# Graph attention, then neighbour quantiles, on one core: the order of scatters, of front pieces and of the first indices is changed

## The chip, the cores and the metric

The kernel runs on one core of a Trainium2 chip. That core has five engines, each with an instruction queue of its own that is worked off in order: TensorE (PE in the profile, its weight loads PEld), VectorE (DVE), ScalarE (ACT), GpSimd (POOL) and SyncE (SP). Transfers between HBM and the on-chip memories are issued from a queue of SP, ACT or POOL. The metric is the device time of one execution in microseconds (us). Semaphores order the engines; a framework places them from the tiles that instructions read and write, and also chooses, at compile time, the order of instructions in each queue.

## The reference, cut to what matters

Two layers follow each other. The first is dense graph attention with 8 heads on 4096 nodes of 128 values, masked by an adjacency matrix of about 1.6% ones, then an output projection and a layer norm:

```python
Wh = jnp.einsum('nd,hde->hne', nodes, W)
e = leaky_relu(f1[:, :, None] + f2[:, None, :])        # f1, f2: Wh times a1, a2
att = softmax(where(adj > 0, e, -9e15))
h = elu(einsum('hnm,hmd->hnd', att, Wh))
x = layernorm(nodes + elu(cat(h) @ W1 + b1))           # (4096, 128)
```

The second layer takes, for each node and each of the 128 features, the three quartiles over the values of the node's neighbours (of which a few, by rank, are left out), averages them, mixes them half and half with the node's own value, and applies one linear layer with a residual:

```python
svals = jnp.sort(where(keep[:, :, None], x[None], big), axis=1)
agg = sum(take(svals, ceil(q * n_keep) - 1) for q in (0.25, 0.5, 0.75)) / 3
out = (0.5 * agg + 0.5 * x) @ W.T + b + x
```

## The kernel before

The kernel makes use of the sparse graph: a node has some 50 to 100 neighbours. Nodes are handled 128 at a time (32 tiles), one per partition. There are three kinds of work.

**The front** (`Front`, from L318) turns the adjacency matrix into lists. `scan` loads quarter rows (`a_i`, 512 KB, SP's queue, L378), ScalarE makes signs of them, TensorE packs 16 columns into a word. `first` and `second` (DVE: rounds of eight maxima and their replacement, L188 and L190) draw the neighbours' numbers out of the words. Tiles come in six blocks of 4, 4, 6, 6, 6 and 6 (`BLOCKS`). `place` sorts the nodes of a block by their degree: it computes a place for each node (`pos_i`, L518), and POOL scatters the lists to those places in HBM (`rows_d`, L541). `keep` writes a row `meta_d` of indices for the second layer. At the end, `order` computes the places over all 4096 nodes, and `late`, 32 scatters from POOL of 512 bytes each, writes `order_d` (L680). The front is cut into 88 pieces in a list `todo`; `advance(n)` takes the next n, and `through(b)` all up to the `place` of block b.

**Attention** (`gat`, from L797) goes in 64 halves of 64 nodes. A node has 8 partitions, so a half is 4 groups of 16 nodes. For each group, gathers from POOL (`nb`, L971) of 128 rows of 136 values each, 28 to 44 gathers for a half and 2190 in all, bring the neighbours' rows from `xf_d`; their indices come from `rows_d` through `ids`, `others` and `info` on SP. Gathers are issued three halves ahead, into six buffers of 18 rows. DVE and ACT make logits and probabilities (L1054 to L1088), DVE spreads them (L1103), TensorE sums the rows (`ps_z`, L1111), and every four halves `combine` computes projection, `elu` and layer norm, one stage of it in each of the halves that follow. It ends in two scatters of the result into `x1_d` (L1197), which the profile calls `x_d`. Each half of the loop ends with `advance(2)`. The loop takes `late` in behind the last gather of the program's text, but a scatter of `late` depends on the front alone, so the framework may place it earlier.

**Quantiles** (`sparse`, from L1675) go by tiles of 128 nodes, sorted by degree. POOL fetches the tile's `info` row, the nodes' own values `xs`, and 50 to 100 neighbour rows (`rows`, L1713; three tiles of buffers). DVE sorts the rows with a network of compares (`compare`, L1738). A compare of k pairs is one ACT copy of the lower rows to PSUM (tile `low`, two of them[...]; up to 4 pairs to `low_s` in SBUF) at L1751, then a minimum and a maximum on DVE (L1756, L1757). `interleave` orders the steps of the end of tile t-1 and the beginning of tile t. `plan` makes the steps, of at most 16 pairs, 8 in the first part of tile 0. When a tile is sorted, `pick` lets ACT scale 2 to 14 candidate rows (`picked`, L1810), lets TensorE sum them into the last quarter of a `low` tile that a compare of at most 12 pairs is using (`sums`, L1815 and L1818), and ACT copies the sum out. Every fourth tile, `finish` does the linear layer likewise (`layer`, L1837) and scatters the output. These small jobs stand in the list `waiting`; each compare takes one.

Between the two layers, a flag is read and a branch taken: a graph that doesn't fit the bounds takes a dense path. Nothing after the branch is placed ahead of it.

Of the kernel before, what the change touches and what calls it, by code (L numbers as in the profile page):

```python
# [38 lines left out]
F32 = mybir.dt.float32  # L39
F16 = mybir.dt.float16  # L40
BF = mybir.dt.bfloat16
I32 = mybir.dt.int32
# [3 lines left out]
ALU = mybir.AluOpType  # L46
# [4 lines left out]
P = 128  # L51
N = 4096
D = 128
# [36 lines left out]
SMALL = 4  # L90
FOUR = 4
CUT = 32
MOST = 16

ENDS = [(t - t % FOUR, FOUR) for t in range(NT - FOUR)]
ENDS += [(NT - FOUR, FOUR - 1)] * (FOUR - 1) + [(NT - 1, 1)]
# [697 lines left out]
    return out  # L794


def gat(tc, nc, c, x, adj, xf_d, meta_d, order_d, flag_d, w, a1, a2, w1, b1, gamma, beta, x1_d):  # L797

# [22 lines left out]
    with ExitStack() as ctx:  # L823
# [3 lines left out]
        def advance(count):  # L827
            while todo and count > 0:
                name, piece = todo.pop(0)
                piece()  # L830
                count -= name != "open"
# [299 lines left out]
        def combine(t, zT):  # L1131
# [62 lines left out]
            nc.vector.tensor_add(s, s, bc["beta"].unsqueeze(1).to_broadcast(shape))  # L1194
            yield
            for j in range(TWO):
                nc.gpsimd.indirect_dma_start(  # L1197
                    out=x1_d,
                    out_offset=bass.IndirectOffsetOnAxis(ap=index[t + j][3][:, 0:1], axis=0),
                    in_=s[:, j, :],  # L1200
                    in_offset=None,
                )

        held = {u: load(u) for u in range(3)}
        advance(EARLY)
        f1s = {0: spread_f1(0)}
# [3 lines left out]
        for u in range(2 * NT):  # L1210
            t, half = divmod(u, 2)
            if u + 3 < 2 * NT:
                held[u + 3] = load(u + 3)
            elif late:

                advance(len(todo))
                for piece in late:
                    piece()
                late = []
            if not half and t + 1 < NT:  # L1220
                f1s[t + 1] = spread_f1(t + 1)
            ps_z, behind = rows_sum(u, held.pop(u), e)
            if u + 1 < 2 * NT:
                with ExitStack() as order:
                    for ins in behind:
                        order.enter_context(tc.issue_after(ins))
                    e, behind = probabilities(u + 1, held[u + 1], f1s[(u + 1) // 2])
            with ExitStack() as order:
                for ins in behind:
                    order.enter_context(tc.issue_after(ins))  # L1230
                if u % (2 * TWO) == 0:
                    zT = tp.tile([P, H, TWO * P], F32, name="zT")
                collect(u, ps_z, zT)
                for stages in going:
                    next(stages, None)
            if u % (2 * TWO) == 2 * TWO - 1:
                going = going[-1:] + [combine(t - 1, zT)]
            advance(2)
        for stages in going:
            for _ in stages:  # L1240
                pass
        advance(len(todo))


def statistics(tc, nc, c, f_sb, f2m, rows_d):
# [412 lines left out]
def plan(t):  # L1658

    wide = HIGH[t]  # L1660
    extra = wide - MAIN if MAIN < wide <= 80 else 0
    w = wide - extra
    needed = {i - 1 for lo, hi in places(t) for i in range(lo - extra, hi + 1)}
    layers = needed_swaps(swap_layers(w), needed)
    merge = (w - 1).bit_length()

    first = steps(layers[:-merge], lambda i: i, PAIRS if t else PAIRS // 2)
    second = steps(layers[-merge:], lambda i: i)
    if extra:
        apart = needed_swaps(swap_layers(extra), range(extra))  # L1670
        first += steps(apart, lambda i: MAIN + extra - 1 - i)
    return first, second, extra


def sparse(tc, nc, c, x1_d, meta_d, order_d, w, b, out):  # L1675


    with tc.tile_pool(name="sp1", bufs=1) as one, tc.tile_pool(
# [12 lines left out]
        sixth = one.tile([P, P], F32, name="sixth_i")  # L1691
        nc.scalar.mul(sixth, c["idf"], 0.5 * float(np.float32(1.0 / NQ)))
        wT = one.tile([P, D], F32, name="lwT")
        it = one.tile([P, 2 * MIDDLE], I32, name="it_p")
        nc.gpsimd.iota(it, pattern=[[1, 2 * MIDDLE]], base=0, channel_multiplier=0)
        iota_p = one.tile([P, 2 * MIDDLE], F32, name="iota_p")
        nc.vector.tensor_copy(iota_p, it)
        order = one.tile([P, NT], I32, name="order")
        for i in range(4):
            nc.sync.dma_start(  # L1700
                out=order[:, ts(i, NT // 4)],
                in_=order_d[ts(i, N // 4), :].rearrange("(t p) c -> p (t c)", p=P),
            )

        def bank():
            return psum.tile([P, PAIRS * D], F32, name="low")

# [2 lines left out]
        nc.scalar.copy(wT, ps[:, :D])  # L1710

        def gather(row, info, col):
            nc.gpsimd.indirect_dma_start(  # L1713
                out=row,
                out_offset=None,
                in_=x1_d,
                in_offset=bass.IndirectOffsetOnAxis(ap=info[:, col : col + 1], axis=0),
            )
# [19 lines left out]
        def compare(rows, step):  # L1738


            shape, d, low, high, _ = step
            lows, highs = block(rows, shape), block(rows, shape, d)
            if low and high:
                _, n2, _, n, _, run = shape
                k = n2 * n * run
                if k > SMALL:
                    t = bank()
                else:
                    t = tp.tile([P, SMALL * D], F32, name="low_s", bufs=4)
                packed = block(t, (0, n2, n * run, n, run, run))  # L1750
                nc.scalar.copy(packed, lows)  # L1751
                if waiting and waiting[0][0] == "copy":
                    waiting.pop(0)[1]()
                elif waiting and SMALL < k <= PAIRS - FOUR:
                    waiting.pop(0)[1](t[:, (PAIRS - FOUR) * D :])
                nc.vector.tensor_tensor(lows, packed, highs, op=ALU.min)  # L1756
                nc.vector.tensor_tensor(highs, packed, highs, op=ALU.max)  # L1757
            elif low:
                nc.vector.tensor_tensor(lows, lows, highs, op=ALU.min)  # L1759
            else:  # L1760
                nc.vector.tensor_tensor(highs, lows, highs, op=ALU.max)
# [41 lines left out]
        def pick(found, x1, comT):  # L1803

            made = {}

            def scale():
                made["v"] = tp.tile([P, MOST, D], F32, name="picked", bufs=1)
                for i, (v, weight) in enumerate(found):
                    nc.scalar.mul(made["v"][:, i, :], v, weight)  # L1810

            def sums(ps):
                made["ps"] = ps[:, :P]
                for i in range(len(found)):
                    nc.tensor.matmul(  # L1815
                        made["ps"], made["v"][:, i, :], sixth, start=i == 0, stop=False
                    )
                nc.tensor.matmul(made["ps"], x1, half, start=False, stop=True)  # L1818

            return [  # L1820
                ("copy", scale),
                ("bank", sums),
                ("copy", lambda: nc.scalar.copy(comT, made["ps"])),
            ]

        def finish(xs, comT, infos):
# [3 lines left out]

            def layer(ps):
                made["ps"] = ps
                for j in range(m):
                    to = ps[:, ts(j, D)]
                    nc.tensor.matmul(to, c["idf"], xs[:, j, :], start=True, stop=False)
                    nc.tensor.matmul(to, c["ones"][0:1, :], b_row[:, j, :], start=False, stop=False)
                    nc.tensor.matmul(to, comT[:, j, :], wT, start=False, stop=True)  # L1837

            def layer_copy():
                o = tp.tile([P, FOUR, D], F32, name="o")  # L1840
# [15 lines left out]
        def load(t):  # L1856
            rows = three.tile([P, max(HIGH), D], F32, name="rows")
            first, _ = ENDS[t]
            if t == first:
                group[first] = (  # L1860
                    tp.tile([P, FOUR, D], F32, name="xs"),
                    tp.tile([P, FOUR, P], F32, name="comT"),
                    [],
                )
            info = three.tile([P, MW], I32, name="info", bufs=3 * FOUR)
            group[first][2].append(info)
            nc.gpsimd.indirect_dma_start(
                out=info,
                out_offset=None,
                in_=meta_d,  # L1870
                in_offset=bass.IndirectOffsetOnAxis(ap=order[:, t : t + 1], axis=0),
            )
            gather(group[first][0][:, t - first, :], info, NODE)
            for s in range(HIGH[t]):
                gather(rows[:, s, :], info, s)
            return rows, info

        plans = [plan(t) for t in range(NT)]
        held = {0: load(0), 1: load(1)}
        for t in range(NT + 1):  # L1880
# [372 lines left out]
def gnn(tc, x, adj, w, a1, a2, w1, b1, gamma, beta, lw, lb, out):  # L2253
    nc = tc.nc
    with ExitStack() as ctx:
# [6 lines left out]

        keep = ctx.enter_context(tc.tile_pool(name="keep", bufs=1))
        c = constants(nc, keep)
        gat(tc, nc, c, x, adj, xf_d, meta_d, order_d, flag_d, w, a1, a2, w1, b1, gamma, beta, x1_d)
        other = nc.values_load(flag_d[0:1, 0:1], min_val=0, max_val=1)
        with tc.If(other > 0) as cmp:
            general(tc, nc, c, x, adj, w, a1, a2, w1, b1, gamma, beta, lw, lb, x1_d, out)
        with cmp.Else():
            sparse(tc, nc, c, x1_d, meta_d, order_d, lw, lb, out)  # L2270


_INS = [
# [33 lines left out]
```

## Time and profile before

| | us |
|---|---|
| timed runs, median of 3 | 8430.65 (8417.16 to 8433.3) |
| profiled execution | 7646.96 |
| its span, from the first to the last instruction | 7645.2 |
| places of the first block ready, first gathers | 133 |
| end of the last gather of attention | 3106.6 |
| last scatter of `x1_d` issued | 3158.4 |
| first row gather of quantiles | 3170.6 |
| first compare | 3187.1 |
| last scatter of the output | 7641 |

The profiled execution is 784 us shorter than the median of the timed runs. All durations that follow are those of the profiled execution. A line of a group of instructions gives the line in the kernel, the engine, the operation and the tiles it writes and reads; a waiting row gives what waited for what, us in total, times, and the longest. The releaser of a wait is inferred. Idle time counts only on the engine that bounds a stage.

### The profile page before, as it was taken

Reading aid. Unit: us, or ns where it says so; the run is one execution under the profiler, and the core shown is the slowest. Engines: PE = TensorE matmul, PEld = TensorE weight load, DVE = VectorE, ACT = ScalarE, POOL = GpSimd, SP = SyncE. Lnnn points to the kernel's source line nnn. Section 1 sums busy time; section 2 is a strip of 40 time slices with the busy share of each in tenths; the row PEclk is TensorE's granted clock in tenths of the full one; section 3 lists DMA queues with packets and bytes.
Section 4 is the critical chain, followed back from the end, with each engine's and each line's share of the span. In section 5 each row is a group of like instructions: output and inputs, shape, how many; then the busy total and the mean of one; then the engine's idle time right before and its main releaser. Section 6 shows DMA issues by size and latency. Waiting matters only on the chain. (4 is left out here: it accounts for less than half of the span.)

```text
span 7645.2 us, 31290 instructions
## 1 busy us (share of the span) xinstructions
PE 1122.8 (15%) x6047; PEld 946.8 (12%) x6047; DVE 5831.7 (76%) x9380; ACT 2214.1 (29%) x2301; POOL 4343.5 (57%) x4524
## 2 busy tenths in 40 slices
PE   3243333322222322100000000000000000000001
PEld 1232222222222222100000000000000000000000
DVE  8465555565223222399999999999999999999999
ACT  6020212100000000144344343434334433443433
POOL 2777677777777777565554645455536434554500
PEclk5566666666566666655555555555555555555555
DMA  6242324222222222111111111111101101111100
GB/s 205 57 121 56 107 62 121 60 55 56 47 56 56 56 56 56 40 44 34 40 35 30 41 31 37 30 36 34 38 23 41 34 24 33 36 35 29 33 1 1
DMA packets 219057, 380.95 MB, mean 50 GB/s; under 512 B 129283, under 2 KB 129412, under 8 KB 218852
## 3 DMA queue, kind: packets, MB, share of 16 engines
q0 software_dynamic: 145808, 308.58, 15.3%
q1 hardware_dynamic: 72898, 70.23, 3.1%
q14 instruction: 156, 1.28, 0.1%
q8 instruction: 49, 0.80, 0.0%
q10 hardware_dynamic: 146, 0.07, 0.0%
HBM read 368.26 MB, written 10.31 MB: 50 GB/s over the span
## 5 line engine op out<-in xcount | busy, mean ns | idle before, releaser
L1713 POOL DMA_INDIRECT rows<-x_d,info x2078 | 2018.2, 971 | 1949.5 <-ACT picked L1810 1270.8
L971 POOL DMA_INDIRECT nb<-xf_d,ids x2190 | 2086.0, 953 | 707.0 <-issue 632.2
L1751 ACT COPY low<-rows 128x2048 f32<-128x2048 f32 (+8 forms) x1022 | 1561.5, 1533 | 2429.9 <-DVE rows L1757 1780.7
L1756 DVE TENSOR_TENSOR rows<-low,rows 128x2048 f32<-128x2048 f32 (+9 forms) x1022 | 1884.7, 1862 | 138.9 <-ACT low L1751 50.0
L1757 DVE TENSOR_TENSOR rows<-low,rows 128x2048 f32<-128x2048 f32 (+9 forms) x1022 | 1882.4, 1861 | 5.8
L1054 DVE TENSOR_TENSOR e<-nb,ps_small 128x64 f32<-128x64 f32 (+9 forms) x200 | 47.7, 240 | 1252.6 <-DMA nb<-xf_d,ids 1206.7
L1111 PE MATMUL ps_z<-spread,nb 128*128 128x128 f32 x4500 | 615.7, 305 | 797.9 <-DVE spread L1103 775.6
L1111 PEld LDWEIGHTS ps_z<-spread,nb 128*128 128x128 f32 x4500 | 604.5, 220 | 829.9 <-DVE spread L1103 420.7
L1815 PE MATMUL low<-sixth_i,picked 128*128 128x128 f32 x300 | 79.8, 442 | 4224.7 <-ACT low L1751 3736.4
L1815 PEld LDWEIGHTS low<-sixth_i,picked 128*128 128x128 f32 x300 | 66.8, 324 | 4237.7 <-ACT low L1751 3744.8
L1073 ACT ACTIVATE ps_e<-e 128x256 f32<-128x256 f32 (+4 forms) x64 | 26.1, 408 | 1936.2 <-DVE e L1054 972.6
L1103 DVE TENSOR_TENSOR spread<-e,ps_small 128x1152 f32<-128x1152 f32 (+4 forms) x312 | 342.7, 1107 | 129.2 <-PE ps_z L1111 79.4
L1845 POOL DMA_INDIRECT out<-o,info x32 | 34.4, 1076 | 392.9 <-ACT o L1841 369.2
L380 ACT ACTIVATE nz<-a_i 128x1024 bf16<-128x1024 int32 x128 | 134.3, 1051 | 292.5 <-DMA a_i<-in_adj 254.3
L1751 ACT COPY low_s<-rows 128x512 f32<-128x512 f32 (+3 forms) x325 | 139.8, 471 | 130.5 <-DVE rows L1756 48.0
L389 PE MATMUL ps_words<-nz,pows 128*128 128x512 bf16 (+1 forms) x272 | 113.7, 577 | 364.4 <-ACT nz L387 258.0
L188 DVE MAX8 k<-key 128x8 f32<-128x256 f32 x416 | 164.6, 412 | 0.7
L1756 DVE TENSOR_TENSOR rows<-low_s,rows 128x512 f32<-128x512 f32 (+3 forms) x325 | 158.3, 500 | 3.0 <-ACT low_s L1751 2.1
L1757 DVE TENSOR_TENSOR rows<-low_s,rows 128x512 f32<-128x512 f32 (+3 forms) x325 | 158.7, 500 | 0.3
L190 DVE MATCH_REPLACE8 key<-k,key 128x256 f32<-128x256 f32 x384 | 155.5, 407 | 0.0
L1142 PE MATMUL ps_h<-zT,w_ga 128*128 128x256 f32 x256 | 116.3, 619 | 198.4 <-DVE s L1414 106.6
L1759 DVE TENSOR_TENSOR rows<-rows 128x256 f32<-128x256 f32 (+8 forms) x245 | 141.6, 580 | 0.2
(246 smaller groups left out, 2528.0 us busy)
## 6 DMA issues: line engine op xcount, KB each, us to landing
a_i<-in_adj SPq DMA_DIRECT2D x128, 512.0 KB
nb<-xf_d,ids POOLq DMA_INDIRECT x2190, 2.5
rows<-x_d,info POOLq DMA_INDIRECT x2078, 2.5
xf_d<-xf POOLq DMA_DIRECT2D x4, 576.0 KB, 7.4
xf<-in_x POOLq DMA_DIRECT2D x4, 512.0 KB
meta_d<-rowdata_k SPq DMA_DIRECT2D x4, 324.0 KB
abc_ta<-in_L_gnn_a POOLq DMA_DIRECT2D x2, 512.0 KB, 7.7
w_ga<-in_L_gnn_W POOLq DMA_DIRECT2D x2, 512.0 KB
```

Source lines behind the costliest of these rows:

```text
L188: nc.vector.max(out=top, in_=work)
L190: nc.vector.match_replace(out=work, in_to_replace=top, in_values=work, imm_value=gone)
L380: nc.scalar.activation(nz[:, j, :], a_i, AF.Relu, scale=-1.0, accum_out=self.negative[:, k : k + 1],)
L971: gather = nc.gpsimd.indirect_dma_start(out=rows[:, used + i, :], out_offset=None, in_=xf_d, in_offset=bass.IndirectOffsetOnAxis(ap=ids[:, ...
L1103: last = nc.vector.tensor_tensor(spread[:, :m], e[:, at : at + m, :].unsqueeze(2).to_broadcast(shape), own.unsqueeze(1).unsqueeze(3).to_br ...
L1111: product = nc.tensor.matmul(ps_z[:, g, :], rows[:, k, :D], spread[:, i].rearrange("p j h -> p (j h)"), start=i0 + i == 0, stop=i0 + i == ...
L1713: nc.gpsimd.indirect_dma_start(out=row, out_offset=None, in_=x1_d, in_offset=bass.IndirectOffsetOnAxis(ap=info[:, col : col + 1], axis=0),)
L1751: nc.scalar.copy(packed, lows)
L1756: nc.vector.tensor_tensor(lows, packed, highs, op=ALU.min)
L1757: nc.vector.tensor_tensor(highs, packed, highs, op=ALU.max)
L1759: nc.vector.tensor_tensor(lows, lows, highs, op=ALU.min)
L1815: nc.tensor.matmul(made["ps"], made["v"][:, i, :], sixth, start=i == 0, stop=False)
```

## The change

- The 32 scatters of `late` are put behind the last gather of attention on POOL.
- The scatters into `x1_d` no longer wait for one another; each node has a row of its own.
- `advance` takes three pieces at the end of each of the first 16 halves, two thereafter.
- `order` and the first two `info` rows are loaded inside `gat`, between the last but one and the last `combine`, into tiles that outlive it; so is the constant `iota_p`. `sparse` no longer makes them.
- In the first part of tile 0, steps have at most 4 pairs instead of 8.
- A compare no longer depends on the matmuls of `sums` or `layer` that use other columns of its PSUM tile.
- `scale` is one piece for each row instead of one for all.
- In `load` of quantiles, everything stands behind the row gathers of the tile before, `xs` behind the rows; `info` has 10 buffers instead of 12, and `picked` 14 rows instead of 16.

```diff
@@ gat
             for j in range(TWO):
-                nc.gpsimd.indirect_dma_start(
+                done = nc.gpsimd.indirect_dma_start(
                     out=x1_d,
...
                 )
-
+                for other in stored:
+                    tc.declare_no_dep(done.ins, other, reason="each node has a row of its own")
+                stored.append(done.ins)
...
                 advance(len(todo))
-                for piece in late:
-                    piece()
+                with tc.issue_after(gathers[2 * NT - 1][HALF - 1, 0]):
+                    for piece in late:
+                        piece()
                 late = []
...
-            advance(2)
-        for stages in going:
+            advance(3 if u < 2 * START[2] else 2)
+        for stages in going[:-1]:
             for _ in stages:
                 pass
-        advance(len(todo))
+
+        for i in range(4):
+            nc.sync.dma_start(
+                out=order[:, ts(i, NT // 4)],
+                in_=order_d[ts(i, N // 4), :].rearrange("(t p) c -> p (t c)", p=P),
+            )
+        for t, info in enumerate(infos):
+            nc.gpsimd.indirect_dma_start(
+                out=info,
+                out_offset=None,
+                in_=meta_d,
+                in_offset=bass.IndirectOffsetOnAxis(ap=order[:, t : t + 1], axis=0),
+            )
+        for stages in going[-1:]:
+            for _ in stages:
+                pass
@@ plan
-    first = steps(layers[:-merge], lambda i: i, PAIRS if t else PAIRS // 2)
+    first = steps(layers[:-merge], lambda i: i, PAIRS if t else PAIRS // 4)
@@ sparse, compare
+                aside = []
                 if waiting and waiting[0][0] == "copy":
                     waiting.pop(0)[1]()
                 elif waiting and SMALL < k <= PAIRS - FOUR:
-                    waiting.pop(0)[1](t[:, (PAIRS - FOUR) * D :])
-                nc.vector.tensor_tensor(lows, packed, highs, op=ALU.min)
-                nc.vector.tensor_tensor(highs, packed, highs, op=ALU.max)
+                    aside = waiting.pop(0)[1](t[:, (PAIRS - FOUR) * D :])
+                for to, op in ((lows, ALU.min), (highs, ALU.max)):
+                    done = nc.vector.tensor_tensor(to, packed, highs, op=op)
+                    for product in aside:
+                        tc.declare_no_dep(done.ins, product, reason="other columns of the bank")
@@ sparse, load
-            info = three.tile([P, MW], I32, name="info", bufs=3 * FOUR)
-            group[first][2].append(info)
-            nc.gpsimd.indirect_dma_start(
...
-            gather(group[first][0][:, t - first, :], info, NODE)
-            for s in range(HIGH[t]):
-                gather(rows[:, s, :], info, s)
+            with ExitStack() as after:
+                if gathered:
+                    after.enter_context(tc.issue_after(gathered[-1]))
+                if t < len(infos):
+                    info = infos[t]
+                else:
+                    info = three.tile([P, MW], I32, name="info", bufs=2 * FOUR + 2)
+                    nc.gpsimd.indirect_dma_start(
...
+                for s in range(HIGH[t]):
+                    done = gather(rows[:, s, :], info, s)
+                gather(group[first][0][:, t - first, :], info, NODE)
+                gathered.append(done.ins)
```

`tc.issue_after(ins)` puts the instructions of its block behind `ins` in the same engine's queue; `tc.declare_no_dep(a, b)` takes away the dependence of `a` on `b`.

## The prediction

> **What bounds the kernel now.** I read the page first, then the stage table, then the waits of the bounding engine in each stage, then the timeline of the crossing between them.
>
> The page's slices show two regimes: VectorE partly idle in the first 17, full in the rest.
>
> ```profile
> PE 1122.8 (15%) x6047; PEld 946.8 (12%) x6047; DVE 5831.7 (76%) x9380; ACT 2214.1 (29%) x2301; POOL 4343.5 (57%) x4524
> ...
> DVE  8465555565223222399999999999999999999999
> ...
> POOL 2777677777777777565554645455536434554500
> ```
>
> In the stage table (stretch, length, then busy time and count for PE, PEld, DVE, ACT, POOL):
>
> ```profile
> 1911.00:3049.00 1138.00, 313.16 (x1989) 290.53 (x1987) 313.30 (x802) 67.41 (x127) 860.05 (x910) 0.62 0.23 55
> 3310.00:7500.00 4190.00, 136.54 (x488) 110.90 (x488) 4098.18 (x3180) 1673.71 (x1437) 2000.71 (x2055) 0.50 0.12 32
> ```
>
> Attention late on: 910 POOL instructions in 1138 us, 1.25 us each. The timeline has each gather busy 0.94 and idle 0.30 "issue", so POOL is full at 76% busy: attention ends when the gathers have been issued, plus the stalls of POOL. Quantiles: DVE is 97.8% busy. Time comes out of this kernel by taking an instruction or a stall from POOL before the last gather, by shortening the crossing, or by closing DVE's last gaps.
>
> POOL's stalls in attention (waited for: total us, times, longest):
>
> ```profile
> POOL nb L971 <- PE ps_z L1111: 36.9, 8, 21.6
> ...
> POOL me L947 <- DMA info<-rows_d: 12.3, 3, 4.2
> ...
> POOL x_d L1197 <- DMA x_d<-s,info: 10.6, 6, 3.2
> ```
>
> The first is a gather waiting for a buffer because VectorE is late. Why it is late shows in SyncE's timeline and in DVE's waits at the same place:
>
> ```profile
> 778.87 4.17 SPq L903 DMA_DIRECT2D ids<-rows_d  x6
> 783.08 5.75 SPq L919 DMA_DIRECT2D others<-rows_d  x11
> 788.94 19.71 SPq L378 DMA_DIRECT2D a_i<-in_adj  x8
> ```
> ```profile
> DVE ps_e L1074 <- ACT ps_e L1073: 39.4, 1, 39.4
> ```
>
> SP stood at `ids` until POOL's scatters of block 2 (770 to 778), though their places were ready at 711; the adjacency pieces queued behind came at 789; ScalarE, in order, held a scan ahead of the logits; DVE lost 39 us, then POOL 8.5 and 21.6 us.
>
> The crossing:
>
> ```profile
> 3105.62 0.94 POOL L971 DMA_INDIRECT nb<-xf_d,ids  x1 [0.30 <-issue]
> ...
> 3146.65 0.98 POOL L1197 DMA_INDIRECT x_d<-s,info  x1 [40.09 <-DVE s L1194]
> ...
> 3158.36 0.96 POOL L1197 DMA_INDIRECT x_d<-s,info  x1 [2.55 <-DMA x_d<-s,info]
> ...
> 3162.97 0.99 POOL L1867 DMA_INDIRECT info<-meta_d,order  x1 [0.72 <-issue]
> ...
> 3170.57 0.94 POOL L1713 DMA_INDIRECT rows<-x_d,info  x1 [0.30 <-issue]
> ...
> 3187.05 0.96 DVE L1756 TENSOR_TENSOR rows<-low,rows 128x768 f32<-128x768 f32 x1 [20.10 <-DMA rows<-x_d,info]
> ```
>
> From the last gather's end (3106.6) to the first row gather of quantiles: 64.0 us, in which POOL sits idle for 40.
>
> DVE's gaps after 3310:
>
> ```profile
> DVE rows L1756 <- ACT low L1751: 44.9, 45, 1.9
> DVE rows L1756 <- PE low L1837: 20.3, 8, 3.3
> DVE rows L1756 <- PE low L1818: 12.3, 10, 2.2
> ```
>
> [...] the matmuls of `sums` and `layer` write its last quarter and the compare beside them uses 12 rows, the first three. So the 18 waits above (32.6 us) order things that needn't be, and I count them as gone. [...] the forecast for attention goes by where instructions stand in each queue.
>
> **The change part by part**, against the profiled execution (7646.96 us, span 7645.2). The median of the timed runs is 8430.65, 784 us more; nothing in this trace says where that lies.
>
> (1) Late scatters. In the order before, all 32 of `order_d` stand between gathers 1297 and 1347 of 2190; in the changed order, behind the 2190th. They cost POOL 32 x 1.256 = 40.2 us ahead of the last gather; there they now stand in the 40.1 us hole. Gain 40.
>
> (2) Free scatters of `x_d`. The second of each pair waited 1.53 us, where 0.30 is normal: eight such in attention, with one of 3.2, make some 10 us.
>
> (3) Three pieces per half in the first 16 halves. No work is added; DVE's front work moves earlier, and the POOL order with it. I gave each DVE instruction of the changed order the mean by which its kind advances DVE in this trace, and counted POOL's at 1.249 us from the first scatter at 133:
> - block 1: DVE needs 122 us, POOL arrives after 207;
> - block 2: DVE 196 more, POOL 229 later (scatter behind gather 333, at 569);
> - block 3: DVE 200 more, POOL 237 later (behind gather 507, at 807);
> - blocks 4 and 5: DVE 207 and 233, POOL 295 and 336.
>
> So DVE keeps up, at 86% where it is tightest (62% before). Its in-order waits matter too: the places of block 2 come 57 us of DVE work behind the logits of half 7, whose gathers end at about 497: 558, against 569. Those of block 3 come 55 us behind half 13 (gathers end 750): 806, against 807. I allow 3 us there. Behind a waiting scatter stand all later gathers, and on SP `ids` and the adjacency pieces, so this is the place to watch. In return the scatters come when their places are ready, rather than 59 us later (block 2), and SP lets the scan through: pieces issued behind block 2's scatter are needed by half 10, whose gathers end only at 617. Of the 36.9 us of buffer stalls I keep 6: gain 31. The waits of 4.1 us for `info` follow a pair of stores on which SP waits to refill that buffer; two of three stay: gain 4.
> Sum for attention: 40 + 10 + 31 + 4 - 3 = 82 us. From both sides: 40 (each stall comes back as another) to 100; and below nothing, see the rivals.
>
> (4) Indices ahead. The 32 scatters end 40 us after the last gather, land 3.6 later (median of that DMA), the loads of `order` take SP 2.4 and then some 2.4 to land (taken from `info`, the nearest row), the two `info` gathers 2.5, and four stores, whose last values are ready at 48, 5: 54 to 56 instead of 52.8. Then the branch (2.7) and rows at once; five `info`, one `xs` and the iota (8 us) are gone: 58 instead of 64. Gain 6. If that cover were gone (stores ready sooner), the chain through `order` would be late next.
>
> (5) First tile in steps of 3 or 4 pairs: the first compare needs 6 rows, not 12: 7.5 us sooner. But its last row lands 62 us after its first in either kernel, and tile 1's rows, which DVE met 2 us after they landed, become the next limit. Gain 5, between 0 and 8; the steps add some 4 us of DVE work inside waits.
>
> (6) The 18 waits for PE: gain 30 of 32.6. Between 0 and 33: ACT's copy out of the bank could take the wait over, but DVE is two compares, over 4 us, away from that bank.
>
> (7) Scaling piece by piece, `xs` and `info` behind the rows, buffers 12 to 10, MOST 14: nothing. ACT's order of scales and copies is almost the same in both, so row buffers come free at the same points; POOL has a mean 45 us of idle (1270.8 / 28) ahead of each tile's gathers, and rows land 17 us or more before first use in all but tiles 1 and 31. If the releases did come one compare (4.4 us) later, tile 31 would feel it alone.
>
> Sum: 82 + 6 + 5 + 30 = 123: 7524 in a profile. If the 784 us of the timed runs stretch all stages alike (1.10), it is 135. I take 130: 8300.
>
> **Rivals.**
> (A) Attention wins only the scatters and half the stores' waits (45): a buffer stall or a wait at `rows_d` of 30 to 40 us replaces the old ones. For it: margins of 1 and 11 us at two scatters. Against: DVE has 155 us unused before block 3's. Gain 86: 8345. Chance 0.22.
> (B) Attention as forecast, the PE waits return as waits for ACT: gain 93: 8338. For it: the ACT row is already the largest. Chance 0.12.
> (C) Slower: DVE's idle share doesn't shrink. From 133 to 711 it was busy 347.5 of 578 us. If it idles 40% on, its 518 us of work take 863, block 3's places come at 996 instead of 806, POOL stalls 190 us at that scatter, and the time is 8430.65 + 190 - 123, about 8500. It decides once the two stalls at blocks 2 and 3 pass 123 us together. Against: part of that idling was the blocked scan, which goes, and the rest was VectorE waiting for gathers with no front piece placed ahead. Chance 0.09, of which 0.04 stalls that just eat the gain.
> (D) The timed runs lose more than the profile where POOL bounds, and gains there grow: 8250. Chance 0.10.
> (E) The change does not do what it says, the scatters still ahead of the gathers or on the way out: the order of instructions excludes the first; the second costs at most the 40, gain 83, 8348. Chance 0.05.
> The forecast, 8275 to 8325, has 0.42.
>
> **Numbers.** Time 8300; range 8245 to 8375, which leaves out the tail of D and C. A measurement of this kernel can tell about 0.2% (17 us). Faster 0.91, same 0.04, slower 0.05.
>
> **What would show it.** Last gather near 3025 (3107 before); no `order_d` scatter among gathers; no wait of `x_d` for `x_d`; POOL's wait at `rows_d` under 15 us for blocks 2 and 3 (more says A or C); rows of tile 0 begin 58 us after the last gather; the two rows "<- PE low" gone from DVE's waits and the ACT row no larger than 50 (else B). The forecast is wrong if DVE's front work meets POOL at the scatters, or if the unseen 784 us depend on the order of transfers.

## The result and the profile after

The changed kernel is slower: 8545.69 us (median of 4 runs, 8537.73 to 8555.35) against 8431.97 for the kernel before on the same chip, ratio 1.0138 (95% interval 1.0120 to 1.0156), 114 us. The forecast was 8300.

One thing has to be said for the numbers to be understood: the kernel before takes 7643 to 7655 us in some sessions on a chip and 8377 to 8440 in others (one chip showed both), all kernels of a session move together, the profile that the forecast was made from is of the first kind and the timed runs given with it of the second. I call them the 7647 setting and the 8430 setting, and compare only with the kernel before in the same session.

The profile after is of the 8430 setting (span 8535.9 us). The page, busy time first, then the slices:

```profile
PE 1224.0 (14%) x6047; PEld 1018.7 (12%) x6047; DVE 5890.0 (69%) x9454; ACT 2221.7 (26%) x2338; POOL 4346.9 (51%) x4524
...
DVE  6454564553222222225898979899899998999999
...
POOL 3545546566666666656254534536454435444410
```

Busy times are those of the kernel before within some 100 us; the span is not. VectorE is no longer at 9 in every slice of the quantiles, and POOL no longer at 7 in attention. The stage table, with the same two stretches as in the prediction:

```profile
1911.00:3049.00 1138.00, 344.37 (x1821) 300.61 (x1822) 312.07 (x863) 63.06 (x120) 753.63 (x794) 0.60 0.20 50
3310.00:7500.00 4190.00, 278.01 (x1238) 233.41 (x1236) 3470.49 (x3000) 1407.79 (x1285) 2088.55 (x2152) 0.51 0.12 34
```

POOL issues 794 instructions in the first stretch, where 910 had been: it is not the bound of attention here. (The second now begins inside attention, so its VectorE time cannot be set beside the old one.) The waits of POOL, then of VectorE:

```profile
POOL nb L973 <- PE ps_z L1113: 455.5, 28, 58.5
...
POOL nb L973 <- remote: 197.1, 42, 9.2
POOL rows_d L541 <- DVE pos_i L518: 84.8, 4, 58.0
```
```profile
DVE spread L1105 <- remote: 593.8, 42, 46.4
...
DVE rows L1769 <- ACT low L1762: 197.0, 31, 45.0
...
DVE k L188 <- remote: 129.5, 57, 3.1
```

The buffer stall that the forecast cut from 36.9 us to 6 is 455.5. "remote" is a semaphore that rose when no recorded instruction had just ended: the instruction that was waited for is in the record as finished, and its signal came later, in this trace 1.5 to 51.4 us after the last recorded end of the engine that raises it. (Of matmuls the profile's own legend says that their ends are modelled.) In the first profile of the kernel before, no wait carries that word. The crossing, on POOL and then VectorE:

```profile
3714.05 0.95 POOL L973 DMA_INDIRECT nb<-xf_d,ids  x1 [0.30 <-issue]
3715.30 0.99 POOL L680 DMA_INDIRECT order_d<-node,pos_g  x1 [0.30 <-issue]
...
3754.56 0.96 POOL L680 DMA_INDIRECT order_d<-node,pos_g  x1 [0.30 <-issue]
...
3787.75 0.99 POOL L1199 DMA_INDIRECT x_d<-s,info  x1 [23.63 <-DVE s L1196]
...
3802.40 0.98 POOL L1724 DMA_INDIRECT rows<-x_d,info  x1 [4.22 <-issue]
```
```profile
3811.32 1.15 DVE L1769 TENSOR_TENSOR rows<-low_s,rows 128x384 f32<-128x384 f32 x2 [11.90 <-DMA rows<-x_d,info]
```

The order of instructions is what the diff says: 32 scatters behind the last gather, stores at once one behind the other, rows 4.2 us after the last store. But the last gather ends at 3715.0, not near 3025, and the crossing takes 87.4 us.

### The profile page after: what moved, and what is told of

The parts are those of the page before. It is cut to its first block, busy times and chain, and to the rows that moved or that the text cites. A ratio compares the mean times of both kernels' runs of the same rounds, so it can differ in the third digit from the quotient of the medians.

```text
span 8535.9 us, 31472 instructions
## 1 busy us (share of the span) xinstructions
PE 1224.0 (14%) x6047; PEld 1018.7 (12%) x6047; DVE 5890.0 (69%) x9454; ACT 2221.7 (26%) x2338; POOL 4346.9 (51%) x4524
## 5 line engine op out<-in xcount | busy, mean ns | idle before, releaser
L1769 DVE TENSOR_TENSOR rows<-low,rows 128x2048 f32<-128x2048 f32 (+10 forms) x1970 | 3650.7, 1893 | 264.7 <-ACT low L1762 197.0
L1762 ACT COPY low<-rows 128x2048 f32<-128x2048 f32 (+8 forms) x985 | 1528.4, 1557 | 2312.0 <-DVE rows L1769 1697.4
L1113 PE MATMUL ps_z<-spread,nb 128*128 128x128 f32 x4500 | 740.3, 320 | 1450.2 <-issue 708.4
L1113 PEld LDWEIGHTS ps_z<-spread,nb 128*128 128x128 f32 x4500 | 687.0, 233 | 1524.1 <-issue 974.5
L1769 DVE TENSOR_TENSOR rows<-low_s,rows 128x512 f32<-128x512 f32 (+3 forms) x798 | 395.4, 523 | 129.3 <-remote 38.9
L188 DVE MAX8 k<-key 128x8 f32<-128x256 f32 x416 | 169.1, 416 | 177.0 <-remote 125.7
L1128 ACT COPY zT<-ps_z 128x512 f32<-128x512 f32 x64 | 37.6, 588 | 901.3 <-remote 752.4
L1762 ACT COPY low_s<-rows 128x512 f32<-128x512 f32 (+3 forms) x399 | 179.6, 486 | 287.2 <-DVE rows L1769 176.4
L188 DVE MAX8 lists<-cand 128x8 f32<-128x176 f32 x416 | 127.6, 332 | 65.6 <-remote 33.3
```

Source lines behind the costliest of these rows:

```text
L188: nc.vector.max(out=top, in_=work)
L1113: product = nc.tensor.matmul(ps_z[:, g, :], rows[:, k, :D], spread[:, i].rearrange("p j h -> p (j h)"), start=i0 + i == 0, stop=i0 + i == ...
L1769: done = nc.vector.tensor_tensor(to, packed, highs, op=op)
```

## The experiments

All times are medians; the ratio is to the kernel before in the same session, with its interval.

| kernel | 7647 setting | ratio | 8430 setting | ratio |
|---|---|---|---|---|
| before, again | 7647.51 | 1.0 (0.9992 to 1.0009) | 8424.32 | 0.9999 (0.9987 to 1.0011) |
| changed | 7531.4 | 0.985 (0.9833 to 0.9866) | 8545.69; 8563.01 | 1.0138; 1.0167 (1.015 to 1.0184) |
| attention edits alone | 7580.95 | 0.9913 (0.9896 to 0.9929) | | |
| quantile edits alone | 7603.04 | 0.9941 (0.9924 to 0.9957) | | |
| late scatters alone | 7609.29 | 0.9951 (0.9935 to 0.9968) | | |
| changed, two pieces | 7543.62 | 0.9865 (0.9849 to 0.9882) | 8423.29 | 1.0043 (1.0029 to 1.0057) |
| the same, steps of 8 | | | 8354.29 | 0.9959 (0.9945 to 0.9973) |
| the same, later front | 7515.64 | 0.9824 (0.9808 to 0.9841) | | |
| the same, layer by 2 tiles | 7505.38 | 0.9811 (0.9794 to 0.9827) | 8323.27 | 0.9884 (0.9868 to 0.9901) |

Which setting a session has could not be chosen, so empty cells were not measured.

### The parts, and the kernel before once more

The kernel before, unchanged:

> The kernel before, unchanged, to have a profile of an execution of the usual length. Theory S (slow stretches): the 784 us between the profile shown (7647) and the timed runs (8431) are stretches of 20 to 45 us in which one engine issues an instruction only every 0.7 or 1.4 us, as TensorE does in 28 stretches of the changed kernel (655 us). Then this run gives 8431, and its profile has such stretches on TensorE of at least 400 us in all, and idle time of POOL in attention well above the 74 us of the profile shown. Rival U (uniform): the 784 us are spread over all work (longer instructions, longer gathers); then no group of instructions is waited for by 100 us more than in the profile shown.

Before, with the attention edits (`issue_after` around `late`, the free stores, and three pieces):

```diff
-            advance(2)
+            advance(3 if u < 2 * START[2] else 2)
```

> Before, with the three edits of attention alone: late scatters behind the last gather, free scatters of x1, three front pieces per half in the first 16 halves. Theory F (the loss is made in attention): about 8540, as the whole change. Rival Q (the loss is made in the quantiles): 8300 to 8400, with the gain that was forecast for attention (82). Rival S (slow stretches decide, wherever they fall): anything between, with a TensorE or ScalarE stretch behind most of POOL's idle time.

Before, with the hunks of `plan`, `compare`, `pick`, `finish` and `load`, the indices staying where they were:

> Before, with the edits of the quantiles alone: finer steps in tile 0, compares free of the matmuls, scaling in pieces, info and xs behind the rows, fewer buffers; order and the first indices stay where they were. Theory F: 8390 to 8430. Rival Q: 8520 to 8600.

The changed kernel with one line taken back:

```diff
-            advance(3 if u < 2 * START[2] else 2)
+            advance(2)
```

> The changed kernel with two front pieces per half throughout. If the three pieces make the loss: 8340 to 8430, below the kernel before. If they are neutral: 8546, as the changed kernel. If they are what the forecast took them for (a gain of 31): 8570 to 8580.

The session had the 7647 setting: 7647.51, 7580.95, 7603.04 and 7545.55. The times expected were those of the 8430 setting, so none of them came, and theories S and U were not tested. Nothing loses here: attention gains 66 us, the quantiles 44, and all but the third piece 102. Theories F and Q, a loss made by one part wherever it runs, fall. Whether it was the setting or the kernel, the next run asked:

> The changed kernel, unchanged, beside the kernel before on a chip (the three runs of parts were made where the kernel before takes 7647). Theory S (slow stretches made the loss, and they belong to where the first comparison ran): without stretches the forecast's own sum holds, 7524 (123 below 7647), last gather near 3025, three pieces 20 to 30 faster than two (7546). Rival L (the changed kernel itself loses): 7720 to 7770, 1.4% above the kernel before, as in the first comparison. If the kernel before takes 8430 here again, the stretches of both can be set side by side: S then expects some 200 us more of them in the changed kernel.

The kernel before took 8429.14 there, and the changed one 8563.01. So the loss is real and can be repeated in that setting. Then both beside each other, with two more:

> The changed kernel, unchanged. Where the kernel before takes 7647: 7520 to 7530 (theory S; parts measured so far there: attention 66, quantiles 44, all but the third piece 102 below), last gather near 3042. Where it takes 8430: 8545 to 8565, as twice before.

> Before, with the late scatters alone put behind the last gather. Where the kernel before takes 7647: 40 less, 7607, as step 1 of the forecast has it; if the scatters come back on the way into the quantiles (they stand ahead of the last stores and of the loads of order): 7620 to 7647. Where it takes 8430: 8390 if POOL still bounds the end of attention, 8430 if TensorE does.

Late scatters alone are this in the kernel before:

```diff
-                for piece in late:
-                    piece()
+                with tc.issue_after(gathers[2 * NT - 1][HALF - 1, 0]):
+                    for piece in late:
+                        piece()
```

7647 setting again: the changed kernel takes 7531.4, 116.6 us less than the kernel before (7647.96), and the late scatters alone 38.7 less. Rival L, a changed kernel that loses in itself, falls. The kernel before, run once more among them, took 7647.38, and the changed kernel with two pieces 7543.62. From the trace of the changed kernel, the waits (POOL, then VectorE) and the crossing:

```profile
POOL nb L973 <- PE ps_z L1113: 33.5, 12, 24.3
```
```profile
DVE spread L1105 <- PE ps_z L1113: 133.7, 74, 39.0
...
DVE rows L1769 <- ACT low L1762: 37.5, 41, 2.8
```
```profile
3043.18 0.94 POOL L973 DMA_INDIRECT nb<-xf_d,ids  x1 [0.30 <-issue]
3044.42 0.99 POOL L680 DMA_INDIRECT order_d<-node,pos_g  x1 [0.30 <-issue]
...
3083.62 0.95 POOL L680 DMA_INDIRECT order_d<-node,pos_g  x1 [0.31 <-issue]
3092.40 1.09 POOL L1256 DMA_INDIRECT info<-meta_d,order  x1 [7.83 <-DMA order<-order_d]
...
3098.89 0.96 POOL L1199 DMA_INDIRECT x_d<-s,info  x1 [0.30 <-issue]
3102.32 0.98 POOL L1724 DMA_INDIRECT rows<-x_d,info  x1 [2.48 <-ACT lwT L1721]
```

No row says "remote"; the last gather ends at 3044.1, the rows begin 58.2 us behind it, the rows "<- PE low" are gone and the one for ACT fell from 50.0 to 37.5. This is the execution that was forecast (7524), but for the last gather, which was to come at 3025.

### What the 8430 setting is in the trace

> The kernel before, unchanged, once more: its profile has been 7647 in three looks, while the two comparisons that found the changed kernel slower had it at 8430. If it takes 8430 here: theory S has stretches of slow issue on VectorE, TensorE and ScalarE, fewer of them than the changed kernel's (655 us on TensorE), about 600 us lost in attention and 200 in the quantiles, last gather at 3600 to 3750; theory F' (the changed kernel loses in attention alone): quantiles as long as the changed kernel's 4720 from the last gather to the end, or longer; theory Q' (it loses in the quantiles alone): last gather where the changed kernel has it, 3729. If it takes 7647 it tells nothing of this.

It took 8424.32. Set against the first profile of the same kernel, the trace (span 8438.4) loses 588 us up to the last gather (3694.3 for 3106.6), nothing from there to the first compare (80.8 for 80.5), and 205 from there to the last scatter (4660 for 4455). POOL's waits for buffers, and VectorE's longest in the quantiles:

```profile
POOL nb L971 <- PE ps_z L1111: 418.3, 32, 37.0
...
POOL nb L971 <- remote: 192.1, 36, 10.1
```
```profile
DVE rows L1756 <- remote: 192.6, 8, 42.2
```

Where there had been 36.9 us in the first of these rows and nothing in the others, there are now 803; the spans differ by 793. Theory U, a loss spread over all work, falls. Theory S holds in kind: TensorE's row sums idle on "issue" here, 164.7 us from 143 to 1411 and 143.7 from 3310 to 3690 (708.4 in the whole trace of the changed kernel in the first comparison, no row in the first profile of the kernel before). Neither F' nor Q' holds alone (the 4720 of F' counts from the first compare): against this trace, the changed kernel's first one loses 21 us up to the last gather, 16 in the crossing (96.3 to the first compare) and 61 from there to the last scatter (4722). TensorE at the linear layer of one group of tiles, then VectorE at the same place:

```profile
4857.38 0.79 PE L1836 MATMUL low<-lb,ones 1*128 1x128 f32 x2
4858.10 0.80 PE L1837 MATMUL low<-lwT,comT 128*128 128x128 f32 x2
```
```profile
4853.86 2.16 DVE L1756 TENSOR_TENSOR rows<-low,rows 128x1920 f32<-128x1920 f32 x1 [1.83 <-ACT low L1751]
4898.20 1.09 DVE L1756 TENSOR_TENSOR rows<-low,rows 128x896 f32<-128x896 f32 x1 [42.18 <-remote]
```

The last matmul is recorded as done by 4858.9; the compare that waits for it starts at 4898.2, and the record of the semaphore has its last five rises at 4888.3, 4893.9, 4896.0, 4898.1 and 4898.2. Since a matmul's end is modelled, the trace doesn't tell whether the work or only its signal came late. Meanwhile POOL issued a row gather each 1.25 us, as ever. In attention TensorE itself goes slow behind a burst (changed kernel, first comparison):

```profile
3308.75 3.18 PE L1113 MATMUL ps_z<-spread,nb 128*128 128x128 f32 x27
...
3319.99 0.37 PE L1113 MATMUL ps_z<-spread,nb 128*128 128x128 f32 x1 [2.43 <-issue]
...
3343.09 0.37 PE L1113 MATMUL ps_z<-spread,nb 128*128 128x128 f32 x1 [0.33 <-issue]
3343.79 0.37 PE L1113 MATMUL ps_z<-spread,nb 128*128 128x128 f32 x1 [0.33 <-issue]
```

27 matmuls in 3.2 us, and then one in each 0.7 to 3.5 us, nearly all with nothing waited for. VectorE shows it in the front's small instructions ("k L188 <- remote", 2.3 us each before a MAX8 of 0.4 us); the semaphore that they wait for is VectorE's own, and it rose 1.6 to 3.0 us after the last recorded end on VectorE (changed kernel, first comparison), so late signals aren't a matter of modelled ends alone. ScalarE shows it in the quantiles (725.7 us of its idle time before `low` are "issue", where the first profile of the kernel before has no such row). POOL doesn't: its gathers keep 1.25 us. The places are the program's, not chance: in two executions of the changed kernel the eight long waits of VectorE in the quantiles are 26.8, 24.5, 45.0, 27.7, 20.0, 33.8, 22.6, 17.5 and 26.8, 24.4, 45.0, 27.7, 20.5, 33.2, 25.4, 17.5 us.

### Where the loss is

Gather 750 of 2190 is a mark that all kernels pass. The stage table from the first gather to it, in the 8430 setting for the kernel before, the changed one, and the changed one with two pieces:

```profile
142.90:1410.80 1267.90, 347.06 (x1676) 279.91 (x1675) 600.59 (x2499) 184.89 (x295) 749.80 (x787) 0.59 0.29 72
```
```profile
143.00:1533.60 1390.60, 338.48 (x1720) 271.58 (x1720) 737.61 (x3176) 230.70 (x362) 759.06 (x792) 0.59 0.27 75
```
```profile
142.40:1391.70 1249.30, 339.07 (x1674) 275.41 (x1673) 598.20 (x2497) 184.35 (x295) 750.68 (x787) 0.59 0.30 73
```

In the 7647 setting, for the kernel before and the changed one:

```profile
143.50:1175.30 1031.80, 320.81 (x1744) 258.22 (x1743) 585.65 (x2530) 187.48 (x299) 749.49 (x787) 0.62 0.36 89
```
```profile
143.10:1174.40 1031.30, 327.61 (x1749) 261.30 (x1749) 720.15 (x3209) 235.21 (x369) 760.54 (x793) 0.62 0.40 101
```

The third column of work is VectorE. In the 7647 setting the stretch takes 1031 us with 586 or with 720 us of VectorE in it: POOL sets the length, and the third piece is taken from VectorE's idle time (446 us, then 311). In the 8430 setting that idle time is no slack: 667, 653 and 651 us, whatever is put in. Against the kernel before, 137 us more of VectorE's work (737.61 - 600.59) make the stretch 123 us longer; against two pieces it is 139 and 141, of which some 8 (an estimate: 0.56% of the stretch) are that session's own, as the kernel before took 8385 in it and 8432 in the other. What VectorE waited for there, in the kernel before in the 7647 setting and in the 8430 setting:

```profile
DVE e L1054 <- DMA nb<-xf_d,ids: 259.2, 28, 22.5
```
```profile
DVE den L1039 <- issue: 99.2, 6, 49.2
DVE spread L1103 <- remote: 93.4, 6, 29.7
DVE k L188 <- remote: 89.8, 40, 3.4
```

Gathers, in the first; late signals and slow issue, in the second, where the row for gathers is among the small ones (under 17.5 us). And what POOL waited for, before and changed in the 8430 setting:

```profile
POOL nb L971 <- PE ps_z L1111: 230.8, 15, 37.0
```
```profile
POOL nb L973 <- PE ps_z L1113: 333.5, 17, 58.5
```

TensorE's sums waited 191.5 us for VectorE's `spread` in the kernel before and 289.1 in the changed one. Back from the row sums, that is the chain: VectorE late, spread late, sums late, buffer late. Those buffer stalls grow by 103 us, the ones put down to "remote" shrink by 21 (31.8 to 10.7), and stores that wait for VectorE add 34 (27.6 and 6.7). From gather 750 on, the changed kernel returns only part: 2180 us to the last gather, 2210 with two pieces, since from gather 1350 on all of them go at one pace (1219 before, 1219 changed, 1213 with two pieces; 1074 in the 7647 setting), where TensorE's sums are late: in the changed kernel POOL's gathers wait there for 118.2 us on "remote", in 22 waits.

The kernel with two pieces, which took 7545.2 in one more session of the 7647 setting, met this one here:

> The changed kernel with two front pieces per half, again, to meet the setting in which the kernel before takes 8430. There, theory F'' (three pieces bunch VectorE's small instructions): gather 750 at 1390 to 1430, last gather 3640 to 3690, total 8470 to 8510. Rival G (the other edits cost the lag): last gather 3700 to 3730, total 8530 to 8560. Where the kernel before takes 7647: 7545.

8423.29, ratio 1.0043 where three pieces have 1.0138 and 1.0167: the third piece costs 0.95 to 1.24%, 80 to 104 us. Gather 750 comes at 1392, as theory F'' has it; the last ends at 3602.5 (3715.0 with three), and that and the time are some 40 us below its ranges, in a session in which the kernel before is faster too (8385 for 8430). Theory F'' holds in kind; rival G falls.

The other taken-back edit, in the same session:

```diff
-    first = steps(layers[:-merge], lambda i: i, PAIRS if t else PAIRS // 4)
+    first = steps(layers[:-merge], lambda i: i, PAIRS if t else PAIRS // 2)
```

> The changed kernel with two front pieces per half and with the steps of at most 8 pairs back in tile 0. Where the kernel before takes 8430: if the finer steps make VectorE's small waits (74 us more of them than before), 55 to 75 less than two pieces alone, 8400 to 8450; if they do not, the same as two pieces alone. Where it takes 7647: 7545 to 7552, since the finer steps were worth about 5.

8354.29: the finer steps cost 69 us here. The first 224 us from the first compare, changed kernel and then this one:

```profile
DVE rows L1769 <- remote: 38.9, 18, 3.2
DVE rows L1769 <- issue: 32.8, 23, 2.7
DVE rows L1769 <- DVE rows L1769: 24.9, 30, 1.5
```
```profile
DVE rows L1769 <- issue: 9.7, 12, 2.0
DVE rows L1769 <- DVE rows L1769: 6.4, 7, 1.5
DVE rows L1769 <- remote: 3.7, 2, 2.0
```

96.6 us in 71 waits against 19.8 in 21: behind the 71, compares of 0.4 to 0.8 us (one of 1.8) start 0.7 to 3.9 us after the one before. What is left of the change gains 30 us there (ratio 0.9959).

### A version that beats both

Pieces moved the other way, with steps of 8 as above:

```diff
-            advance(3 if u < 2 * START[2] else 2)
+            advance(2 if u < 12 or u % 2 else 1)
```

> Two front pieces per half in the first 12 halves, then two and one by turns; steps of 8 pairs in tile 0; else the changed kernel. It moves the front the other way than the change did. Where VectorE is late in early attention and the kernel before takes 8385 to 8430 (theory F''): the front's later pieces fall where VectorE waits for row sums, so 20 to 80 less than with two pieces (0.4% below the kernel before): 0.6 to 1.4% below it. Rival G' (the order of pieces is worth nothing, the third one was a special case): again 0.4% below. Where the kernel before takes 7647: POOL bounds either way, 7545 to 7560.

The same, and the linear layer for two tiles at a time (the columns in `low` stay where they were, four buffers for `xs`, `comT` and `o`):

```diff
-FOUR = 4
+FOUR = 2
...
-                elif waiting and SMALL < k <= PAIRS - FOUR:
-                    aside = waiting.pop(0)[1](t[:, (PAIRS - FOUR) * D :])
+                elif waiting and SMALL < k <= PAIRS - 4:
+                    aside = waiting.pop(0)[1](t[:, (PAIRS - 4) * D :])
```

> The same, and the linear layer of the quantiles for 2 tiles at a time instead of 4 (24 records on TensorE in a row instead of 48). Where the kernel before takes 8385 to 8430 there are eight waits of 17 to 45 us behind the 48 matmul records of a linear layer, 190 to 220 us in all. If the length of the burst makes the wait (theory B): 120 to 200 us less than the kernel above, near 2 to 3% below the kernel before. Rival R (the total of records makes it): no less. Where the kernel before takes 7647: no such waits, and within 10 us of the kernel above.

7647 setting: 7515.64 and 7505.38. That the later front gains 30 over two pieces there was in neither theory: the last gather ends 30 us sooner (3027.6 for 3057.7), and 21 of them are buffer stalls, which fell from the first row (two pieces) to the second.

```profile
POOL nb L973 <- PE ps_z L1113: 45.0, 11, 25.4
```
```profile
POOL nb L973 <- PE ps_z L1113: 24.0, 14, 9.5
```

Two repeats of the last kernel stayed in that setting (7503.04 and 7504.76); a third met the other:

> As the run before, a last time, for the setting in which the kernel before takes 8385 to 8430: theory F'' has the last gather 20 to 80 before that of two pieces (3602), rival G' at 3600 to 3610; theory B has waits over 5 us of VectorE in the quantiles below 80 us in all and the time 2 to 4% below the kernel before, rival R 180 or more and 0.6 to 1.4% below. Else 7505.

8323.27, ratio 0.9884. On the front, rival G' comes out at the end: gather 750 at 1372 (1392 with two pieces) and 1350 at 2361 (2388), but the last at 3606; what was moved later was not free there either. That is close, since the kernel before took 8427 beside this kernel and 8385 beside the one with two pieces: scaled by that (an estimate) the last gather would be at 3588, still short of the 3582 of theory F''. So the gain of the later front is shown in the 7647 setting alone. On the burst, neither: VectorE's waits over 5 us in the quantiles, the starts of rows apart, are eight of 7.6 to 26.8 us, 155 in all, where 4 tiles at a time had eight of 12.3 to 44.7, 211 in all. Theory B wanted under 80, rival R 180 or more, and the time is in R's range. From the first compare to the last scatter the smaller layer gains 41 us here and 11 in the 7647 setting. Within the 40 us ahead of such a wait lie mostly 44 records of TensorE, the sums included, where 68 had been. The longest waits did shrink; that the length of a burst alone makes them isn't shown.

## Why the prediction was wrong, point by point

The step that failed is the last of the sum: "If the 784 us of the timed runs stretch all stages alike (1.10), it is 135. I take 130: 8300." In the profile's own setting the sum was right: 7524 forecast, 7531.4 measured, though in part by luck, as attention gave 66 us for 82 and the quantiles 44 for 35. The 784 us are not a stretch of all stages (1.19 up to the last gather, 1.00 in the crossing, 1.05 behind it): they are slow issue and signals that come late behind bursts, they turn VectorE's idle time in early attention into a limit (651 to 667 us idle, whatever is put in), and they make small instructions dear (96.6 us of waits with the finer steps, 19.8 without). Two terms that were gains in the sum are losses there. In the 8430 setting: third piece +80 to +104, finer steps +69, all the rest -30, together 119 to 143; measured 1.38 to 1.67% of 8430, 116 to 141. (The terms are steps of one chain of kernels, so that they add up is no further test of them.)

- (1) Late scatters, 40: 38.7 alone in the 7647 setting. In the 8430 setting, from gather 1200 to 1350 POOL takes 249 us with two pieces and 300 in the kernel before, which has its 32 scatters there; but of these 50, 31 are given back behind the last gather (to the last store 84 us, before 53), since the last row sum now ends 62 us after it instead of 29.
- (2) and (3) Free scatters and three pieces: all of attention was to give 82, and gave 66 in the 7647 setting. The free scatters gave their 10 (last gather at 3067.2 with the late scatters alone, 3057.7 with both). The third piece was mis-sized even there: forecast 28 (31 less 3), measured 12 (7543.6 to 7531.4). Buffer stalls fell from 36.9 to 33.5, not to 6: one of 24.3 at 564 took the place of those of 8.8 and 21.2 at 820 and 881, behind a scan that TensorE, in order, met at 367 ahead of its row sums (VectorE's wait of 39.0). "DVE keeps up, at 86%" used durations of a setting in which VectorE waits for gathers; where the runs were timed it waits for itself.
- (4) Indices ahead, crossing 58: 58.2 in the 7647 setting, the chain through `order` last, as said (7.8 us before `info`). In the 8430 setting 87.4, against 64.3 before.
- (5) Finer steps, 5: the first compare starts 9.0 us after the first row gather instead of 16.5, as forecast, but from the last gather to the last scatter it is 4481 us with them (two pieces) and 4482 without (the later front), so they are worth about 1; in the other setting 69 us are lost.
- (6) Free compares, 30 of 32.6: that a compare and matmuls in other columns of a tile need no order was the author's assumption. The rows are gone, and first compare to last scatter went from 4455 to 4414 us in the 7647 setting ((5) included), by 41, more than the 35 of both, and the row for ScalarE fell too, by 12.5. In the 8430 setting rival B's mechanism is there to see. The kernel before has 192.6 us on "remote" and 40.8 on ScalarE's copies, the changed one 38.9 and 197.0: VectorE no longer waits for TensorE, but for ScalarE, which waits for TensorE to copy the layer out and has the next compare's copy behind that:

```profile
5034.67 0.59 ACT L1865 COPY o<-low 128x512 f32<-128x512 f32 x1 [47.44 <-remote]
...
5036.97 4.22 DVE L1769 TENSOR_TENSOR rows<-low,rows 128x1792 f32<-128x1792 f32 x2 [44.96 <-ACT low L1762]
```

- The rivals: C had the cause right in kind (VectorE's idle time doesn't shrink; it gave 8500) and the place wrong: POOL stalls at the buffers, 333.5 us, and at the scatters 14.2. It had 0.09. D took the unknown 784 us for a gain, and they were a loss. The prediction's own last sentence, that it is wrong if those us depend on the order of transfers, is near to what happened: they depend on the order and size of VectorE's and TensorE's instructions. The mistake is the weight, since a tenth of the time that no trace explains can't be scaled away with 0.05 left for slower.

## What to carry to other kernels

The profiled execution and the timed runs differed by a tenth here (7647 and 8431 us), and the profile showed another condition than the timed one: where that is so, get a trace of the timed kind before costing an edit, or give the other sign a real chance. VectorE's idle time up to gather 750 was slack where its longest waits were for gathers (259.2 us: 446 us idle became 311) and none where they were for late signals and slow issue (667 stayed 653); look at what ends an engine's waits before counting on them. The edits that made instructions smaller, or packed small ones closer together, were the ones that turned in the 8430 setting: the third piece cost 80 to 104 us there, the finer steps 69 (in the 7647 setting they gained about 1). Shorter bursts on TensorE gained in both, 41 us in the 8430 setting and 11 in the other.

## What the runs showed of the hardware

- Two settings, 10% apart, with the same work: busy time of VectorE 5845 and 5890 us, 159 and 49 packets of instructions fetched in both (changed kernel), granted TensorE clock 0.551 and 0.547 (kernel before). So more code loading doesn't make the difference. Nor does the clock: in the quantiles of the kernel before it is 0.50 in both (205 us longer); up to gather 750 it is 0.59 for 0.62, which on TensorE's 347 us of work there makes 17 us (an estimate: 347 x (1 - 0.59/0.62)), of the 236 that the stretch is longer. One chip had both settings, in two sessions.
- In the slower, an engine that has issued a burst goes on slowly: TensorE at 0.7 us or a multiple for each matmul behind 27 in 3.2 us (changed kernel, from 3308.75), VectorE with waits of 2.3 us before a MAX8 of 0.4 us, and with up to 3.9 us from one compare of 0.4 to 0.8 us to the next. At the linear layers, behind 68 records of TensorE within 40 us (34 matmuls and their weight loads), TensorE's semaphore rises 15.8 to 42.4 us after the recorded, modelled end (seven waits of ScalarE, changed kernel; 39.3 us at 4858.9 in the kernel before). POOL's gathers keep 1.25 us.
- Why stays open: no run here shows what holds the engines and their signals up. The delays fall by place and not by chance: of the eight long waits of VectorE in the quantiles, the third is the longest, 45.0 us, in both executions of the changed kernel.
